# A hand-written schedule on one core: the planner's prices for VectorE and ScalarE, the hand-over between engines and the kernel product are changed

## The chip, the cores and the metric

The kernel runs on one core of a Trainium2 chip. The metric is the device time of one execution in microseconds (us), as the median of several. TensorE (PE) does the matrix products, VectorE (DVE) and ScalarE (ACT) work on what it leaves in PSUM, GpSimd (POOL) mostly starts DMAs and SyncE (SP) starts most of the others. Each engine executes its own instructions in the order in which they were written down, and waits on semaphores for the others.

## The reference, cut to what matters

There are 32 graphs of 512 nodes with 256 features. One layer is computed: a normalisation, then three things that feed a recurrent (GRU) cell, and the sum with the input.

```python
h = jnp.maximum(_layernorm(x, axis=-1), 0.0)
# convolution branch: 1 tap, then 17 taps along the nodes
c = jax.nn.relu(_bn(_conv1d(hc, conv1_w, 0), ...))
x_conv = jax.nn.relu(_bn(_conv1d(c, conv2_w, 8), ...) + hc)
# message branch
s = h @ w_se.T + b_se
A = jnp.exp(-dist(s, s)) * adj
x_nmp = jnp.einsum('bnm,bmd->bnd', A, jax.nn.relu(h @ w_msg.T + b_msg))
# gates
gi = concat([x_conv, x_nmp]) @ w_ih.T + b_ih
gh = h @ w_hh.T + b_hh
r, z = sigmoid(gi_r + gh_r), sigmoid(gi_z + gh_z)
out = x + (1 - z) * tanh(gi_n + r * gh_n) + z * h
```

All numbers are float32, and every matrix product is done in float32.

## The kernel before

**The work.** Five kinds of work share the engines. *Begins* normalise a graph and turn it so that features lie on partitions (`hT`), and store that in DRAM (`hd`). *Rows* load `hd` again into `hT`, do the one-tap convolution (`conv1`, PE into a bank `ps_g`, then ACT into `h`). *Conv* is the 17-tap convolution by a fast scheme: 7 groups of columns with 25 products each, 175 in all. DVE makes the operands `x` and `xd`, PE multiplies into the two banks `ps_c`, ACT copies them to `n` and `z`, DVE sums these into `y`, ACT writes `part` and a DMA stores it. *Graphs* make the messages, the matrix `A` and their product (`messages`, `factors`, `kernel_exp`, `masked`, `gather`). *Gates* do the GRU cell in banks `ps_acc`, most of it by Strassen's scheme.

**The order.** It is not left to a scheduler of the framework (`manual_schedule`). Each kind of work is a Python generator that issues a few instructions and then yields the time at which it can go on, or a condition. A planner at the end of the kernel keeps a clock `now`, which is PE's time: `matmul` adds `max(0.223, 0.005 + columns / 600)` us to it and `turn` adds 0.11. Of the generators that can go on, the planner picks the one whose stream is furthest behind, lets it issue, and calls `fill()`, which gives DVE and ACT background work as long as `dve.free < now + 1.5`. Where no generator can go on, `now` is moved by 0.25, and nothing is issued for it except, in the first stage, a transposition by the identity (`keep_warm`, line 147).

So no figure of the planner is a time on the chip. Figures decide only the order of instructions on the engines, and through it who waits.

**The figures.** `Engine` (lines 116 to 130) holds for DVE and ACT the time `free` at which the engine will be through with what it was given. An instruction moves it on:

```python
size = max(elements(t) for t in tiles if hasattr(t, "shape"))
self.free = max(self.free, now) + self.fixed + self.each * size
```

A generator that needs the result usually yields `act.free + LAG` or `dve.free + LAG`. Two places matter for what follows. After the first half of a product, `ps_c` is copied to the other bank by ACT, and the product goes on at `act.free + LAG`. When a product is done, `both` has ACT copy the two banks out one after the other, and what comes next on these banks may go on at `bank_at`, which is set after the first of the two copies:

```python
for k, half in enumerate(ps):
    n = half.shape[-1]
    act.activation(dst[:, k * n : (k + 1) * n], half, AF.Copy)
    if k == 0:
        bank_at = act.free + LAG
```

`kernel_exp` (line 966 and on) does four small matmuls at the same time, in four parts of the array (line 983); in the later stage its first bank is `pair[1]`, the second of the two banks. After them it moves `now` by a constant, and ACT takes the exponential of the four banks.

`load_row` (line 212) loads a graph's `hT` from DRAM; the rows yield until `now + 8.0`. DMA figures of this kind are constants and not touched by the change.

Of the kernel before, what the change touches and what calls it, by code (L numbers as in the profile page):

```python
# [50 lines left out]
def kernel(  # L51
# [31 lines left out]
    nc = tc.nc  # L83
# [22 lines left out]


    now = 5.0
    LAG = 0.6

    def elements(t):
        n = 1
        for k in t.shape[1:]:
            n *= k
        return n

    class Engine:
# [6 lines left out]
        def __getattr__(self, name):  # L124
            def issue(*tiles, **more):
                size = max(elements(t) for t in tiles if hasattr(t, "shape"))
                self.free = max(self.free, now) + self.fixed + self.each * size
                getattr(self.engine, name)(*tiles, **more)  # L128

            return issue  # L130

    dve, act = Engine(nc.vector, 0.12, 0.00108), Engine(nc.scalar, 0.16, 0.0009)

    def matmul(ps, lhsT, rhs, **more):
        nonlocal now
# [17 lines left out]
    def bank():  # L153
        return gps.tile([P, N], F32, name="ps_g")
# [4 lines left out]
    def later(t, f):  # L159
        LATER.append((t, f))  # L160
        LATER.sort(key=lambda e: e[0])
# [74 lines left out]
    def residual(b):  # L236
# [6 lines left out]
        def relu():  # L243
            act.activation(XC[b], XC[b], AF.Relu)
            RES[b] = act.free + LAG

# [104 lines left out]
    def norm(b):  # L351
# [14 lines left out]
        for c0 in range(0, NT, step):  # L366
# [5 lines left out]
            for c in range(c0, c0 + step):  # L372
# [4 lines left out]
                if c % 2:  # L377
                    yield act.free + LAG

# [156 lines left out]
    def weights_first():  # L536
# [10 lines left out]
        for j1 in ORDER:  # L547
# [12 lines left out]
            for j2 in ORDER:  # L560
# [13 lines left out]
                WS.append(w)  # L574
                W_AT.append(act.free + LAG)
                yield 0.0
# [24 lines left out]
    def third_weight(m):  # L601
# [5 lines left out]
        later(dve.free + 0.4, lambda: nc.gpsimd.dma_start(WD[m % 25][:, 2], w[2]))  # L607
        W_AT[m] = dve.free + LAG

# [11 lines left out]
    def summed(g):  # L621
# [23 lines left out]
        def both(dst, ps):  # L645
# [4 lines left out]
            else:  # L650
# [5 lines that stand above are left out]
            sums_at = act.free + LAG  # L656

# [314 lines left out]
    def kernel_exp(at):  # L972

        nonlocal now, bank_at, exp_waits
        exp_waits = False
        if not wide:
            extra = acc.tile([P, N], F32, name="ps_acc")
        else:
            extra = pair[1]
        pss = [extra, bank(), bank(), bank()]  # L980
        for c in range(NT):
            k = slice(32 * c, 32 * c + 5)
            nc.tensor.matmul(  # L983
                pss[c], gr.left[k, :], gr.right[k, :], start=True, stop=True,
                tile_position=(32 * c, 0),
            )
        now += 1.15
        for c in range(NT):
            act.activation(at[:, c, :], pss[c], AF.Exp)

# [95 lines left out]
    def graph(b):  # L1086
# [21 lines left out]
        if in_product:  # L1108
            exp_waits = True
            yield lambda: not in_product  # L1110
            yield bank_at
        kernel_exp(at)
        yield act.free + 0.3
        for n in range(NT):
# [593 lines left out]
```

## Time and profile before

The time is 2064.82 us, the median of 3 runs (2063.84 to 2067.84). The profiled execution took 2067.35 us, with a span of 2065.6 us from its first to its last instruction, so 1.75 us lie around the span; it is 2.5 us above the median.

| engine | busy us | share of the span | instructions |
|---|---|---|---|
| PE | 2012.4 | 97% | 9199 |
| DVE | 1416.3 | 69% | 2626 |
| ACT | 888.4 | 43% | 1805 |
| POOL | 451.1 | 22% | 578 |

| group of instructions | count | busy us |
|---|---|---|
| PE `ps_acc<-xnb,wih` | 772 | 364.4 |
| PE `ps_c<-xd,w` | 2304 | 291.8 |
| PE `ps_c<-x,w` | 2032 | 267.4 |
| PE `ps_g<-at,msg` | 512 | 227.1 |
| ACT `ps_c<-ps_c`, all widths | 144 | 56.1 |

How to read it: a float32 matmul stands in the records as two, so the program's 4796 matmuls and transpositions would be 9592 records, of which 9199 were kept. The mean granted clock of PE was 0.989 of full speed. The name to the left of `<-` is the tile that is written, those to the right are read. An instruction's recorded duration overlaps the next one on the same engine, so its spacing is shorter than its duration.

### The profile page before, as it was taken

How to read it: one execution, taken by the hardware profiler on the slowest of the kernel's cores; microseconds unless marked ns; L12 is line 12 of the kernel's file. 1: busy time of each engine (PE TensorE's matmuls, PEld its weight loads, DVE VectorE, ACT ScalarE, POOL GpSimd, SP SyncE). 2: the span in 40 equal slices, each digit the busy share in tenths (PEclk: the TensorE clock that was granted, in tenths of full speed). 3: DMA queues.
4: the chain of work that ended last, by engine and by line, in shares of the span. 5: the costliest groups of instructions: out<-in, count | busy, mean ns of one | idle time of the engine just before them, and what ended most of it. 6: DMA issues, size and time to landing. Idle time of an engine off the chain costs nothing. (4 is left out here: it accounts for less than half of the span.)

```text
span 2065.6 us, 27386 instructions
## 1 busy us (share of the span) xinstructions
PE 2012.4 (97%) x9199; PEld 1360.9 (66%) x9199; DVE 1416.3 (69%) x2626; ACT 888.4 (43%) x1805; POOL 451.1 (22%) x578
## 2 busy tenths in 40 slices
PE   8999889999999999999999999999999999999998
PEld 4878556676676766677577676667775677664444
DVE  6789378885878848687587775677875777752223
ACT  6554454335543445433454334554334633334221
POOL 2101022321212213122141221231221311114222
PEclk9999999999999999999999999999999999999999
DMA  7455668898979869778789788797886776756554
GB/s 286 150 174 184 225 209 196 192 226 226 223 197 203 190 192 205 201 182 212 183 193 223 172 204 206 164 197 204 207 204 175 189 158 159 173 118 143 63 92 36
DMA packets 581227, 378.70 MB, mean 183 GB/s; under 512 B 457648, under 2 KB 475344, under 8 KB 579952
## 3 DMA queue, kind: packets, MB, share of 16 engines
q1 hardware_dynamic: 419616, 279.02, 49.1%
q0 software_dynamic: 153184, 84.70, 23.9%
q10 hardware_dynamic: 8288, 13.24, 1.7%
q8 instruction: 73, 1.20, 0.2%
q14 instruction: 66, 0.54, 0.1%
HBM read 278.81 MB, written 114.56 MB: 190 GB/s over the span
## 5 line engine op out<-in xcount | busy, mean ns | idle before, releaser
L1218 POOL DMA_DIRECT2D out_dram<-o_sb x252 | 275.9, 1718 | 659.1 <-DVE o_sb L128 628.9
L137 PE MATMUL ps_acc<-xnb,wih 128*128 128x512 f32 (+1 forms) x772 | 364.4, 593 | 0.7 <-DVE ps_acc L128 0.7
L137 PEld LDWEIGHTS ps_c<-xd,w 128*128 128x128 f32 x2304 | 288.6, 191 | 55.0 <-issue 38.9
L137 PEld LDWEIGHTS ps_c<-x,w 128*128 128x128 f32 x2032 | 258.4, 193 | 72.3 <-issue 49.2
L137 PE MATMUL ps_c<-xd,w 128*128 128x135 f32 (+1 forms) x2304 | 291.8, 280 | 7.0 <-ACT ps_c L128 7.0
L137 PE MATMUL ps_c<-x,w 128*128 128x135 f32 (+2 forms) x2032 | 267.4, 281 | 11.4 <-ACT n L128 5.0
L137 PE MATMUL ps_acc<-hTb,whh 128*128 128x512 f32 (+2 forms) x580 | 239.5, 523 | 0.4 <-ACT r L128 0.4
L137 PE MATMUL ps_acc<-xconv,wih 128*128 128x512 f32 (+1 forms) x580 | 238.9, 519 | 0.3 <-DVE ps_acc L128 0.3
L137 PE MATMUL ps_g<-at,msg 128*128 128x512 f32 x512 | 227.1, 593 | 0.8 <-DVE at L128 0.8
L137 PEld LDWEIGHTS ps_acc<-xnb,wih 128*128 128x128 f32 x772 | 142.6, 191 | 115.6 <-issue 108.7
L137 PEld LDWEIGHTS ps_g<-at,msg 128*128 128x128 f32 x512 | 95.4, 190 | 106.4 <-issue 101.1
L137 PEld LDWEIGHTS ps_acc<-xconv,wih 128*128 128x128 f32 x580 | 107.6, 190 | 74.9 <-issue 67.5
L137 PEld LDWEIGHTS ps_acc<-hTb,whh 128*128 128x128 f32 x580 | 104.8, 191 | 78.6 <-issue 71.2
L128 DVE TENSOR_TENSOR msg<-ps_g,bmsg 128x256 f32<-128x256 f32 x128 | 53.7, 420 | 143.5 <-PE ps_g L137 143.1
L128 DVE SCALAR_TENSOR_TENSOR x<-x,x 128x544 f32<-128x544 f32 (+5 forms) x161 | 137.5, 854 | 2.9
L128 DVE TENSOR_TENSOR o_sb<-hTb,r 128x512 f32<-128x512 f32 x63 | 43.3, 687 | 124.1 <-ACT r L128 123.5
L128 ACT ACTIVATE ps_c<-ps_c 128x270 f32<-128x270 f32 (+1 forms) x144 | 56.1, 389 | 167.8 <-PE ps_c L137 167.8
L128 DVE TENSOR_TENSOR x<-x 128x272 f32<-128x272 f32 (+5 forms) x280 | 127.4, 497 | 0.2
L137 PE MATMUL ps_g<-hT,w 128*128 128x512 f32 (+8 forms) x296 | 122.1, 560 | 3.7 <-DMA hT<-hd 2.5
L137 PE MATMUL ps_g<-wmsg,hTg 128*128 128x259 f32 x496 | 123.5, 382 | 0.7 <-DVE aug L128 0.7
L128 ACT ACTIVATE h<-ps_g,bn_shift,bn_scale 128x252 f32<-128x252 f32 (+8 forms) x212 | 86.5, 485 | 73.2 <-PE ps_g L137 73.2
L128 DVE TENSOR_TENSOR xd<-x 128x544 f32<-128x544 f32 (+1 forms) x144 | 102.5, 716 | 14.0 <-PE ps_c L137 13.7
(149 smaller groups left out, 2927.5 us busy)
## 6 DMA issues: line engine op xcount, KB each, us to landing
w<-wd SPq DMA_DIRECT2D x414, 256.0 KB, 3.4
m_sb<-in_adj_dram SPq DMA_DIRECT2D x384, 64.0 KB, 3.8
hT<-hd SPq DMA_DIRECT2D x33, 512.0 KB, 4.4
hd<-hT POOLq DMA_DIRECT2D x32, 512.0 KB, 5.5
hTb<-hd SPq DMA_DIRECT2D x32, 512.0 KB, 4.6
xnb<-nd SPq DMA_DIRECT2D x64, 256.0 KB, 3.0
out_dram<-o_sb POOLq DMA_DIRECT2D x252, 64.0 KB, 4.9
hTg<-hd SPq DMA_DIRECT2D x31, 512.0 KB, 4.3
```

The costliest lines, as they stand in the source:

```text
L128: getattr(self.engine, name)(*tiles, **more)
L137: nc.tensor.matmul(ps, lhsT, rhs, **more)
L1218: nc.gpsimd.dma_start(dst, src, accum_op=ALU.add)
```

## The change

The figures by which the planner counts are replaced. `LAG`, the time from the end of an instruction on DVE or ACT to the moment at which another engine may count on its result, goes from 0.6 to 0.2 us. DVE's fixed part and its part per element go from 0.12 and 0.00108 to 0.066 and 0.00106, ACT's from 0.16 and 0.0009 to 0.05 and 0.00087; and each bias or scale that is given as a tile adds 0.1. After the four matmuls of `kernel_exp` the clock moves on by 1.5 in place of 1.15. No instruction is changed; their order is.

```diff
     now = 5.0
-    LAG = 0.6
+    LAG = 0.2
...
             def issue(*tiles, **more):
                 size = max(elements(t) for t in tiles if hasattr(t, "shape"))
-                self.free = max(self.free, now) + self.fixed + self.each * size
+                given = sum(hasattr(more.get(k), "shape") for k in ("bias", "scale"))
+                self.free = max(self.free, now) + self.fixed + self.each * size + 0.1 * given
                 getattr(self.engine, name)(*tiles, **more)
...
-    dve, act = Engine(nc.vector, 0.12, 0.00108), Engine(nc.scalar, 0.16, 0.0009)
+    dve, act = Engine(nc.vector, 0.066, 0.00106), Engine(nc.scalar, 0.05, 0.00087)
...
                 tile_position=(32 * c, 0),
             )
-        now += 1.15
+        now += 1.5
         for c in range(NT):
             act.activation(at[:, c, :], pss[c], AF.Exp)
```

## The prediction

> **What bounds the kernel now.** I read the page first: busy times, then the waits of PE, then the clock window by window, and last the rows around single waits.
>
> The page gives PE 97% of the span.
>
> ```profile
> span 2065.6 us, 27386 instructions
> PE 2012.4 (97%) x9199; PEld 1360.9 (66%) x9199; DVE 1416.3 (69%) x2626; ACT 888.4 (43%) x1805; POOL 451.1 (22%) x578
> ```
>
> PE is the bound, and the change takes no matmul away except 11 of the `keep_warm` transpositions (4796 to 4785 on PE; 11 x 0.11 = 1.2 us, issued only where PE has nothing else, so nothing). All that can move is where PE waits. PE's busy time by stretches (0 to 300, 300 to 1850, the rest) leaves 27.7, 19.0 and 6.9 us:
>
> ```profile
> 0.00:300.00 300.00, 272.31 (x1525) 201.64 (x1526) 216.18 (x476) 157.98 (x341) 40.11 (x80) 0.95 0.60 206
> 300.00:1850.00 1550.00, 1530.98 (x7177) 1065.47 (x7176) 1135.58 (x2064) 675.21 (x1393) 348.07 (x435) 0.99 0.81 193
> 1850.00:2066.00 216.00, 209.11 (x500) 93.83 (x498) 64.51 (x88) 55.19 (x73) 62.90 (x63) 1.00 0.52 82
> ```
>
> So the first 300 us lose most, the last 200 us nothing before the closing chain. Who is waited for after 300 us (total, times, longest):
>
> ```profile
> PE ps_c L983 <- ACT z L128: 6.7, 3, 4.0
> PE ps_c L137 <- ACT ps_c L128: 4.1, 4, 3.1
> PE ps_g L137 <- DMA hT<-hd: 2.5, 2, 1.2
> ```
>
> The kernel product waiting for the copy `z`, the second half of a product waiting for its copy, and the reload of `hT`. A long wait costs more than itself, as these stretches show (third number: PE busy; the number after POOL's: granted clock):
>
> ```profile
> 565.90:569.30 3.40, 1.20 (x8) 1.00 (x8) 3.30 (x6) 2.75 (x6) 0.90 (x2) 0.99 0.92 235
> 569.30:576.10 6.80, 4.64 (x18) 4.47 (x19) 6.70 (x12) 2.32 (x3) 5.58 (x8) 0.50 1.25 273
> 838.90:842.30 3.40, 0.00 (x0) 0.00 (x0) 3.37 (x3) 3.37 (x5) 3.40 (x4) 1.00 0.85 40
> 842.30:849.20 6.90, 6.83 (x18) 4.05 (x19) 4.41 (x8) 3.88 (x9) 0.25 (x1) 0.51 0.54 49
> ```
>
> After 3.4 us in which PE worked 1.20 or 0.00 us, the clock is 0.5 for 6.8 us: 3.4 us lost on top.
>
> **The change part by part.** *The prices themselves.* DVE instructions of 512 columns start 0.61 to 0.73 us apart in the trace (1006.05, 1006.77, 1007.50, 1008.11 us) and ACT's exponentials 0.49 apart. The old prices said 0.67 and 0.62, the new ones say 0.61 and 0.50. So the new durations are closer to the chip. They remove no work; what they and the smaller `LAG` do is to let PE come back sooner to a result, with less other PE work in between. How much lies in between I counted in the order of the built instructions, before and after, with a 512-column matmul at its spacing of 0.86 us (two records of 0.43).
>
> *First term: nine kernel products that come too early.* In the changed order, 9 kernel products stand one matmul (0.86 us) after the transpositions of their right factor while ACT has still to do `right` and then both copies of a finished product; before, such products had two matmuls (1.72 us) or more. The reason is that `bank_at` is set after the first copy and the kernel product needs the second bank. The old 0.6 covered the second copy, the new 0.2 doesn't. The rows of such a wait:
>
> ```profile
> 784.34 0.68 ACT L128 ACTIVATE z<-ps_c 128x270 f32<-128x270 f32 x2 [2.46 <-DVE y L128]
> 785.08 0.69 PE L983 MATMUL ps_c<-right,left 5*128 5x512 f32 x1 [2.23 <-ACT z L128]
> ```
>
> From the first copy's start to PE's start are 0.74 us. Before that come 0.20 from PE's end to ACT's start and 0.49 for `right` (836.68 to 837.17): 1.43 us, against 0.86 of cover. 9 x 0.57 = **+5.1 us** (2.5 to 6).
>
> *Second term: reloads of `hT`.* A row's `hT` is read from DRAM where the graph's `hd` has just been written. The rows yield for 8.0 us, and the chain is longer (start, length):
>
> ```profile
> 1349.21 4.73 DMA hd<-hT
> ...
> 1353.96 3.56 DMA hT<-hd
> ```
>
> This one made PE wait 1.22 us, another 1.23. In the order before, two reloads plainly have less PE work between the last work ahead of `hd` and the first `conv1` matmul than the chain takes; in the changed order it is seven, because rows come sooner behind the transposition that makes `hT`. 5 x 1.22 = **+6.1 us** (0, if the writes land a little faster or POOL is free; 15, if POOL's adds to `out`, 4.4 us for four, stand ahead of `hd` each time).
>
> *Third term: the copy inside a product.* Here the order changes most: of 144 such copies, 8 had one matmul of cover and 74 had two; now 86 have one and 22 have two. The need, from rows:
>
> ```profile
> 1778.87 1.08 PE L137 MATMUL ps_c<-x,w 128*128 128x135 f32 x8
> ...
> 1780.05 0.38 ACT L128 ACTIVATE ps_c<-ps_c 128x270 f32<-128x270 f32 x1 [0.26 <-PE ps_c L137]
> ...
> 1780.48 0.73 PE L137 MATMUL ps_c<-xd,w 128*128 128x135 f32 x4 [0.53 <-ACT ps_c L128]
> ```
>
> The half product takes 8 x 0.115 = 0.92 us and ends at 1779.79; PE goes on 0.69 us later. One matmul covers that with 0.17 to spare, so as such the edit costs nothing. The cover that hides it is that ACT has nothing else in hand; ACT's copies `n` and `z` wait for DVE 40.7 us in all by their groups (19.0, 11.2, 7.0 and 3.5), 2% of the span, and a hand-over that hits such a wait now lacks one matmul of cover, up to 0.86 us: 86 x 2% x 0.6 = **+1 us** (0 to 9).
>
> *Fourth term: long waits after 300 us.* The order there is another, so those before go: 1.74 and 3.07 us (565 to 571), 2.23 (783), 4.01 (838), 11.1 in all, and two stretches at half clock, 6.8: -17.9 us. Others come. The worst, a third of the way into the second group of columns: DVE's transposition of the next `hT` waits for the last `conv1` matmul that reads the buffer, and behind it on DVE are queued `xd`, a `y` sum, the second transposition and the third weight `w`, for which PE waits: 0.63 + 0.64 + 1.76 + 0.63 + 0.60, with 0.3 for the two hand-overs 4.6 us, under 0.87 us of messages, so 3.7. Just before, a pair of `conv1` matmuls waits 1.2 for its bank, and that much idle time together costs the half clock, 3.4: 8.3. Three more places, where PE waits behind ACT's `part` or DVE's queue, lack 1.8, 1.75 and 2.5 us: 6.1. -17.9 + 8.3 + 6.1 = **-3.5 us** (-14 if the new ones prove covered; +8 if each new one brings the half clock).
>
> The rule of the Trainium skill in "TensorE: Matmul & The Clock Gate", section "Why this matters for your kernels", allows idle gaps of up to some 3 us and counts a full idle window for the fall to half clock. The stretch at 565.90, with 1.20 us of work, fell too. By that rule only the worst of the new waits could fall and the fourth term would keep its lower half; by the row, several can.
>
> *Fifth term: the first 300 us.* Gone: four waits from 255 to 278 us (2.08, 0.74, 2.00, 2.87) and the one at 208 (2.49), with half clock after two of them, 6.8: -17.0. New: hand-overs that lack 2.0 to 2.6 us at five places, 11.6, and one half clock, 3.4. **-2 us** (-9 to +6).
>
> *`now += 1.5`.* Four such matmuls take PE 1.07 us in the rows (785.08 to 786.15), so the planner's clock now runs ahead by 0.43 for each of the 32 graphs, and ACT and DVE are given that much more work than they have time for. Their slack of 31% and 57% takes it up; it is in the terms above where it matters.
>
> Sum: 5.1 + 6.1 + 1 - 3.5 - 2 = +6.7 us. The profiled execution, 2067.35, would become 2074.0; it lies 2.5 above the median, so the median of 2064.8 becomes 2071.5.
>
> **The rivals.** *It is faster* (0.27). Accurate prices might place work so that the long waits go and do not come back. The mechanism is the clock: four stretches at half clock (208, 255, 565, 838) cost 13.6 us, and a schedule whose waits stay under about 2 us in any 3.4 pays none. With the reloads covered (second term 0) and the worst new wait alone left, the sum is 5.1 + 1 - 17.9 + 8.3 - 5 = -8.5: 2056. It decides if `hd` lands in 4.0 us rather than 4.73, and no two new waits fall together. For it: waits of 4 us and more vanish from the order. Against: by the same count over the order, places where PE comes sooner than the chain before it allows rise from 33 to 51.
>
> *No change that can be told* (0.26). The terms have both signs and 3 us less in the second and third bring the sum to within 4 us: 2061 to 2069.
>
> *The change doesn't do what it says* (part of the slower side, 0.13). The figures are then too short, not traced: for the copy in a product the planner now counts 0.29 + 0.20 = 0.49 us where the rows show 0.69. If the 86 short covers are hit more often than 2%, say one in five by 0.5 us, that is 9 us in place of 1, and 2080.
>
> **How the numbers follow.** Slower, by the sum above or by more, has 0.47, no change 0.26, faster 0.27; under 0.2%, 4.1 us, a measurement of this kernel can't tell a change from none. The time is that of the sum, 2071.5. The range takes the bounds of the terms as independent: downwards 2.6, 6, 1, 10.5 and 7, together 14.3; upwards 1, 9, 8, 11.5 and 8, together 18.6. It is drawn in a little at the top, where only the rival of short figures reaches: 2057 to 2085. The slower case alone would be 2069 to 2086.
>
> **What would show it.** Right: PE's waits for `z` and `n` at line 983 rise from 3 to about 10, most of them near 0.6 us; the waits on the DMA `hT<-hd` rise from 2 to between 4 and 7; the copy `ps_c` is rarely waited for in spite of its short cover; a wait of 3 us or more and a half clock stand near 450 us. Wrong: line 983 not among PE's waits, or the clock at full speed all through after 300 us with a PE idle time there below 15 us, which would make it the faster rival; or dozens of small waits on `ps_c`, which would make it the rival of short figures.

## The result, and the profile after

The changed kernel takes 2090.01 us (median of 5 runs, 2086.88 to 2091.11), the kernel before beside it 2067.33 us (2063.84 to 2073.49): a ratio of 1.0107, with a 95% interval of 1.0086 to 1.0127. It is slower, by 22.7 us and not by the forecast 6.7, and 5 us above the range.

The profiled execution took 2090.64 us. Page, busy times:

```profile
span 2088.9 us, 27331 instructions
PE 2022.3 (97%) x9188; PEld 1356.1 (65%) x9188; DVE 1417.3 (68%) x2626; ACT 888.3 (43%) x1797; POOL 448.8 (21%) x578
```

The work of DVE and ACT is what it was; no engine has become a new bound. (The diff adds a line ahead of all these places: L137 is now L138, L128 is L129, L983 is L984.) The windows, PE's busy time first:

```profile
0.00:300.00 300.00, 276.55 (x1529) 200.87 (x1530) 218.53 (x463) 158.53 (x340) 40.12 (x81) 0.96 0.61 205
300.00:1850.00 1550.00, 1513.42 (x7073) 1048.18 (x7072) 1125.47 (x2053) 667.60 (x1369) 342.41 (x433) 0.99 0.81 191
1850.00:2089.00 239.00, 232.39 (x588) 107.00 (x586) 73.31 (x111) 62.16 (x88) 66.25 (x68) 1.00 0.53 86
```

In the first 300 us PE does 4.2 us more than before; in the next 1550 us it does 17.6 less, and a closing stretch 23 us longer is what that costs. So the loss lies after 300 us. There PE is idle for 36.6 us instead of 18.9, and half clock costs 13.7 us instead of 8.5 (each stretch of 3.4 us by the part of the clock that was not granted). PE's waits after 300 us, total, times and longest:

```profile
PE ps_acc L138 <- ACT r L129: 5.9, 4, 5.3
PE ps_g L138 <- DMA hT<-hd: 5.6, 3, 3.2
PE ps_acc L138 <- DVE ps_acc L129: 4.7, 6, 1.7
PE ps_c L138 <- ACT z L129: 4.5, 1, 4.5
PE ps_c L984 <- ACT z L129: 3.3, 8, 0.5
PE ps_c L138 <- ACT ps_c L129: 3.1, 4, 1.5
PE ps_c L984 <- ACT n L129: 2.1, 3, 1.5
```

The kernel product (L984) waits 11 times for 5.4 us, mostly 0.40 each: a small share. The two longest waits, 5.3 and 4.5 us, are for ACT. What held ACT up is in the timeline around the longer one (start, duration, in brackets the idle time before it and who ended it):

```profile
1350.51 4.47 POOL L1219 DMA_DIRECT2D out_dram<-o_sb  x4
...
1352.12 1.34 ACT L129 ACTIVATE part<-y,bn_shift,bn_scale 128x522 f32<-128x522 f32 x1
...
1353.25 2.90 POOL L746 DMA_DIRECT2D cd<-part  x2
...
1360.89 1.00 ACT L129 ACTIVATE part<-y,bn_shift,bn_scale 128x360 f32<-128x360 f32 x1 [6.16 <-DMA cd<-part]
...
1362.91 0.69 ACT L129 ACTIVATE r<-ps_acc,vec 128x512 f32<-128x512 f32 x1
...
1363.65 2.93 PE L138 MATMUL ps_acc<-hTb,whh 128*128 128x512 f32 x3 [5.27 <-ACT r L129]
```

`part` has two buffers. ACT was through with the older one at 1349.67 (start 1348.33, 1.34 us). POOL issues its store only at 1353.25, after four adds to `out` have been started, and it lands at 1360.87, 11.2 us after ACT was through with the buffer. The next `part` waits 6.2 us for that buffer, and `r`, the gate for which PE waits, comes after it on ACT. The planner counts 5.0 us for that store (`PARTS.append(act.free + 5.0)`). At 575.08 it is the same with `z`: `part` waits 5.62 us, then come 4.47 us of `y`, then `z`. ACT's waits for this store, before and after, from the two lists of waits:

```profile
ACT part L128 <- DMA cd<-part: 12.7, 16, 3.0
```

```profile
ACT part L129 <- DMA cd<-part: 29.8, 13, 6.2
```

### The profile page after: what moved, and what is told of

Same layout as the page of the kernel before. It is cut to its first block, busy times and chain, and to the rows that moved or that the text cites. A ratio compares the mean times of both kernels' runs of the same rounds, so it can differ in the third digit from the quotient of the medians.

```text
span 2088.9 us, 27331 instructions
## 1 busy us (share of the span) xinstructions
PE 2022.3 (97%) x9188; PEld 1356.1 (65%) x9188; DVE 1417.3 (68%) x2626; ACT 888.3 (43%) x1797; POOL 448.8 (21%) x578
## 4 chain that ended last, share of the span: by engine, by line
PE 44%; DVE 2%; DMA 2%; issue 1%; POOL 1%; ACT 1%; SPq 0%; DVEq 0%; POOLq 0%; ACTq 0%
PE ps_acc L138 26%; PE ps_c L138 9%; PE ps_g L138 8%; DMA hd<-hT 1%; PE ps_c L984 1%; POOL out_dram L1219 0%; DMA xconv<-cd 0%; DMA hT<-hd 0%; DMA cd<-part 0%; DVE o_sb L129 0%; DVE z L129 0%; POOL cd L746 0%; DVE y L129 0%; PE ps_g L143 0%; DVE st L129 0%
## 5 line engine op out<-in xcount | busy, mean ns | idle before, releaser
L138 PE MATMUL ps_acc<-xnb,wih 128*128 128x512 f32 (+1 forms) x772 | 366.0, 592 | 0.3 <-DVE ps_acc L129 0.2
L138 PEld LDWEIGHTS ps_c<-xd,w 128*128 128x128 f32 x2304 | 285.0, 190 | 54.4 <-ACT ps_c L129 34.0
L138 PEld LDWEIGHTS ps_c<-x,w 128*128 128x128 f32 x2032 | 258.9, 193 | 71.6 <-issue 42.3
L138 PE MATMUL ps_c<-xd,w 128*128 128x135 f32 (+1 forms) x2304 | 291.0, 279 | 3.3 <-ACT ps_c L129 3.1
L138 PE MATMUL ps_c<-x,w 128*128 128x135 f32 (+2 forms) x2032 | 268.5, 281 | 11.0 <-ACT z L129 5.5
L138 PE MATMUL ps_acc<-hTb,whh 128*128 128x512 f32 (+2 forms) x580 | 242.4, 525 | 5.9 <-ACT r L129 5.9
L138 PE MATMUL ps_acc<-xconv,wih 128*128 128x512 f32 (+1 forms) x580 | 240.3, 520 | 1.8 <-DVE ps_acc L129 1.8
L138 PE MATMUL ps_g<-at,msg 128*128 128x512 f32 x512 | 234.2, 607 | 7.3 <-DVE at L129 7.3
L138 PEld LDWEIGHTS ps_acc<-xnb,wih 128*128 128x128 f32 x772 | 140.7, 190 | 109.0 <-issue 101.6
L138 PEld LDWEIGHTS ps_g<-at,msg 128*128 128x128 f32 x512 | 97.8, 195 | 121.2 <-issue 107.7
L138 PEld LDWEIGHTS ps_acc<-hTb,whh 128*128 128x128 f32 x580 | 104.6, 191 | 82.0 <-issue 69.7
L138 PEld LDWEIGHTS ps_acc<-xconv,wih 128*128 128x128 f32 x580 | 106.5, 190 | 75.6 <-issue 66.0
L129 DVE TENSOR_TENSOR msg<-ps_g,bmsg 128x256 f32<-128x256 f32 x128 | 53.8, 421 | 147.3 <-PE ps_g L138 146.9
L129 DVE SCALAR_TENSOR_TENSOR x<-x,x 128x544 f32<-128x544 f32 (+5 forms) x161 | 137.8, 856 | 3.3
L138 PE MATMUL ps_g<-hT,w 128*128 128x512 f32 (+8 forms) x296 | 127.6, 578 | 12.2 <-DMA hT<-hd 9.0
L129 ACT ACTIVATE ps_c<-ps_c 128x270 f32<-128x270 f32 (+1 forms) x144 | 56.0, 389 | 172.6 <-PE ps_c L138 172.6
L138 PE MATMUL ps_g<-wmsg,hTg 128*128 128x259 f32 x496 | 125.8, 384 | 1.7 <-ACT h L129 1.1
L129 DVE TENSOR_TENSOR x<-x 128x272 f32<-128x272 f32 (+5 forms) x280 | 126.9, 499 | 0.2
L129 DVE TENSOR_TENSOR o_sb<-hTb,r 128x512 f32<-128x512 f32 x63 | 43.2, 686 | 113.2 <-ACT r L129 113.2
L129 ACT ACTIVATE h<-ps_g,bn_shift,bn_scale 128x252 f32<-128x252 f32 (+8 forms) x212 | 86.8, 484 | 71.6 <-PE ps_g L138 71.5
L138 PEld LDWEIGHTS ps_g<-wmsg,hTg 128*128 128x128 f32 x496 | 92.3, 191 | 33.3 <-issue 20.3
```

What stands on the lines that cost most here:

```text
L138: nc.tensor.matmul(ps, lhsT, rhs, **more)
```

## The experiments

**Theory and rivals.** The theory formed after the result: it is `LAG`. The old 0.6 us was not only the time from engine to engine; it was also cover for three waits that the planner does not describe: the second copy of `both` ahead of a kernel product (`bank_at` is set after the first), the `part` store behind POOL's adds, and the reload of `hT`, whose write and read take longer than the counted 8.0 us. Rival one: the new durations, or the 1.5 us after `kernel_exp`, cost the time. Rival two: any other order is worse than the old one, which was a lucky draw, and no figure matters by itself.

In the tables, "idle" is PE's idle time after 300 us (in brackets the waits of over 1.4 us), "half clock" what the clock took there, and "`part`" ACT's waits for its store, all from the profile, all in us. Ratios are to the kernel before.

| run | us | ratio (95%) | idle | half clock | `part` |
|---|---|---|---|---|---|
| before | 2067.33 | 1 | 18.9 (11.0) | 8.5 | 12.7 |
| after | 2090.01 | 1.0107 (1.0086 to 1.0127) | 36.6 (21.7) | 13.7 | 29.8 |
| lag06 | 2079.35 | 1.0059 (1.0041 to 1.0076) | 32.9 (22.1) | 11.9 | 24.7 |
| lagonly | 2094.67 | 1.0128 (1.0100 to 1.0155) | 39.2 (29.3) | 18.8 | 18.4 |
| exp115 | 2090.37 | 1.0126 (1.0092 to 1.0160) | 33.9 (23.7) | 13.7 | 13.4 |

### Which figure costs the time

*lag06*: the changed kernel with the old `LAG`, so the new durations and the 1.5 alone.

```diff
-    LAG = 0.2
+    LAG = 0.6
```

> The changed kernel with LAG back at 0.6 us; the new prices and the 1.5 after the kernel product stay. Theory of thin cover (the short hand-over takes the PE work away from between a result and its use): the 23 us come back but for what 1.5 and the prices cost, 2065 to 2072 us, and the eleven waits of 0.4 us at the kernel product are gone. Theory of undescribed waits (ACT's part behind its store, hT behind its write, which no figure covers): little comes back, 2080 to 2090, since prices and not LAG put the part earlier. Theory of a lucky order before (any other figures give a worse order): anything from 2065 to 2095, without relation to the edit.

*lagonly*: the kernel before with the new `LAG` alone.

```diff
-    LAG = 0.6
+    LAG = 0.2
```

> The kernel before with LAG 0.2 us alone; prices and 1.15 as before. Theory of thin cover: most of the loss is here, 2080 to 2092 us, softened a little since the old prices are some 10% too long on DVE and hold PE back by themselves. If the prices carry the loss: 2065 to 2072. Lucky order: no relation, 2065 to 2095.

*exp115*: the changed kernel with the old step after `kernel_exp`.

```diff
-        now += 1.5
+        now += 1.15
```

> The changed kernel with 1.15 in place of 1.5 after the kernel product. The rows show 1.07 us, so the planner's clock runs ahead less. If the constant matters, ACT and DVE are less behind and the time falls by 5 us or more, to below 2085; if it does not, 2086 to 2094. Lucky order: anything within 15 us of 2090, up as well as down.

`lagonly` loses all of it and more, 1.28%; giving the old `LAG` back (`lag06`) brings half of the loss back and no more. Neither time is in the range that the theory of thin cover gave it: 2094.67 lies above 2080 to 2092, and 2079.35 above 2065 to 2072. The middle window of `lagonly` shows where its loss is:

```profile
300.00:1850.00 1550.00, 1511.41 (x7044) 1050.49 (x7043) 1125.75 (x2053) 665.21 (x1372) 342.23 (x431) 0.99 0.81 191
```

PE does 19.6 us less there than before (1530.98), as in the changed kernel. Its waits for `hT` are not more than before (1.6 us against 2.5), so its loss is not one of waits for the reloads. `exp115` changes nothing in the time, though it changes the waits much: the kernel product's waits go from 5.4 to 20.3 us and those for `part` from 29.8 to 13.4. Taking the 1.5 back brings nothing back. The 12 us of `lag06` were left open here: a price of the new durations, or of this one order.

### Describing the three waits

*guards*: the changed kernel, with all three waits given to the planner: the kernel product yields until after the second copy (`sums_at`), the store counts 9.0 us, the reload 11.0.

```diff
-            HR_AT[b] = now + 8.0
+            HR_AT[b] = now + 11.0
...
-        PARTS.append(act.free + 5.0)
+        PARTS.append(act.free + 9.0)
...
-            yield bank_at
+            yield sums_at
         kernel_exp(at)
```

> The changed kernel with three waits described that its figures leave out: the kernel product may go on only after the second copy (sums_at in place of bank_at in graph), a part buffer counts as free 9 us after the evacuation in place of 5, and a reload of hT is due 11 us after its issue in place of 8. Theory of undescribed waits: the 11 waits at the kernel product (5.4 us idle), most of ACT's 29.8 us on the stores of part and PE's 9.0 us on hT go, with half of the half clock: 2065 to 2073 us. Theory of thin cover at large: only those places get better, 2075 to 2085. Lucky order: 2070 to 2095 with new waits at other places.

*g_parts*, *g_reload* and *g_kernel*: the changed kernel with one of these three edits each (the 9.0, the 11.0, and `sums_at`).

> The changed kernel with one of the three waits described: a part buffer counts as free 9 us after the evacuation, not 5. In the changed kernel ACT stood 29.8 us behind stores of part, and PE's two longest waits (4.5 and 5.3 us) with two stretches of half clock and smaller ones came from that. Theory of undescribed waits: ACT's wait on these stores falls below 5 us, PE's waits of 4.5 and 5.3 us go, 2073 to 2080 us. Theory that any change of the order draws a new lot (lucky order before): the stores' wait may go, but the time stays within 2080 to 2098 with other waits.

> The changed kernel with a reload of hT due 11 us after its issue, not 8. Theory of undescribed waits: PE's 9.0 us on hT go below 2, with one stretch of half clock, 2079 to 2084 us. New lot: 2070 to 2098, whatever becomes of the waits on hT.

> The changed kernel with the kernel product held until the second copy too. Theory of undescribed waits: the 11 waits of about 0.4 us at that line (5.4 us) go, 2083 to 2087 us. New lot: 2070 to 2098; the 11 waits go all the same, but other waits decide the time.

*b_guards*: the kernel before with all three.

> The kernel before (LAG 0.6, old prices, 1.15) with all three waits described. Its ACT stood 12.8 us behind the stores of part and its PE 2.5 us on hT, so there is less to win than in the changed kernel. Theory of undescribed waits: 2060 to 2067 us. New lot: 2065 to 2095, as with any other order.

| run | us | ratio (95%) | idle | half clock | `part` |
|---|---|---|---|---|---|
| guards | 2066.29 | 0.9992 (0.9980 to 1.0004) | 29.8 (14.5) | 10.2 | 0.8 |
| g_parts | 2082.01 | 1.0079 (1.0057 to 1.0100) | 31.8 (17.3) | 11.9 | 1.7 |
| g_reload | 2075.89 | 1.0037 (1.0021 to 1.0054) | 33.3 (17.4) | 11.9 | 29.9 |
| g_kernel | 2068.03 | 1.0002 (0.9991 to 1.0014) | 25.3 (12.9) | 5.1 | 28.5 |
| b_guards | 2070.36 | 1.0007 (0.9997 to 1.0017) | 21.0 (11.6) | 10.2 | 1.3 |

With all three edits, the new figures cost nothing any more: 2066.3 against 2090.0. ACT no longer waits for its store, and PE does 7 us more in the middle window than in the changed kernel:

```profile
ACT part L129 <- DMA cd<-part: 0.8, 2, 0.4
```

```profile
300.00:1850.00 1550.00, 1520.14 (x7125) 1053.63 (x7124) 1132.34 (x2053) 671.90 (x1377) 341.25 (x430) 0.99 0.81 192
```

PE's waits for `hT` fall from 9.0 to 0.9 us. Those of the kernel product for its bank `ps_c`, though, do not fall: 6 of them for 6.6 us, one of 4.2, against 11 for 5.4. The same edits do nothing at the old figures (`b_guards`, though its `part` waits too fall from 12.7 to 1.3), so they are worth something only beside the new ones. That speaks for the theory, although it had expected 2060 to 2067 there. More speaks against reading it too neatly. All three single edits miss the range that the theory gave them. They bring 8, 14 and 22 us, 44 in all, where together they bring 24. `g_kernel` alone brings 22 though it can take away only the 5.4 us of waits at L984 and their share of the clock (5 of them for 2.0 us are left); its waits for `part` stay at 28.5 and those for `hT` at 8.4. (`g_reload` does to the reloads what it says: 3 waits for 2.5 us are left.) Each edit also draws a new order, and that is worth some us by itself. How many was measured next.

### The figure, or one order

A figure was moved by little: enough for another order, too little for another meaning. `b_lag058` and `b_lag062` are the kernel before, `a_lag018` and `a_lag022` the changed one, `p_lag058` and `p_lag08` the changed one with larger values.

```diff
-    LAG = 0.6
+    LAG = 0.58      # b_lag058; 0.62 in b_lag062
...
-    LAG = 0.2
+    LAG = 0.18      # a_lag018; 0.22, 0.58 and 0.8 in the others
```

> The kernel before with LAG 0.58 in place of 0.6 us, an edit that describes the chip neither better nor worse, but reorders PE from its first stage on. Theory of systematic figures (what the prices and LAG say decides): within 5 us of before, 2063 to 2073. Theory of a lucky order before (each order is a new lot, and the kernel before is one of the better ones): 2070 to 2090, as lag06 with 2079.

> The kernel before with LAG 0.62. Systematic figures: 2063 to 2073. Lucky order: 2070 to 2090, and not the same as with 0.58.

> The changed kernel with LAG 0.18 in place of 0.2 us. Systematic figures: within 5 us of 2090. New lot: 2066 to 2095, away from 2090 by more than 5 us as likely as not, since the one-word edit at the kernel product gave 2068.

> The changed kernel with LAG 0.22. Systematic figures: within 5 us of 2090. New lot: 2066 to 2095, and not the same as with 0.18. If both of these lie near 2090 and both of before's neighbours near 2067, the lot is refuted.

> New prices and 1.5 with LAG 0.58, neighbour of the run with 0.6 (2079). If the new prices lose by themselves (they take the ten per cent away by which DVE was counted too slow): 2074 to 2084, like that run. If that run was an unlucky neighbour and LAG is all: 2065 to 2073.

> New prices and 1.5 with LAG 0.8. Theory of thin cover, with the sum of price and LAG as what counts: 0.2 more for each hand-over gives back what the shorter prices took (0.06 on DVE, 0.11 on ACT), so 2063 to 2072. If the prices lose in another way (DVE's and ACT's queues filled too full, which LAG can't mend): 2074 to 2085.

| run | us | ratio (95%) | idle | half clock | `part` |
|---|---|---|---|---|---|
| b_lag058 | 2070.24 | 1.0006 (0.9993 to 1.0018) | 17.8 (11.8) | 10.2 | 26.1 |
| b_lag062 | 2070.71 | 1.0006 (0.9995 to 1.0018) | 21.1 (12.4) | 10.2 | 19.1 |
| a_lag018 | 2085.27 | 1.0079 (1.0060 to 1.0098) | 34.9 (21.8) | 17.1 | 36.3 |
| a_lag022 | 2097.62 | 1.0135 (1.0118 to 1.0151) | 37.2 (22.5) | 17.1 | 16.5 |
| p_lag058 | 2066.88 | 0.9989 (0.9980 to 0.9998) | 22.6 (9.7) | 8.5 | 14.8 |
| p_lag08 | 2068.90 | 1.0001 (0.9988 to 1.0013) | 25.7 (14.8) | 11.9 | 29.4 |

Two of the middle windows side by side, `b_lag058` first, then `a_lag022`:

```profile
300.00:1850.00 1550.00, 1532.19 (x7182) 1066.09 (x7181) 1136.94 (x2066) 675.26 (x1397) 349.31 (x436) 0.99 0.81 193
```

```profile
300.00:1850.00 1550.00, 1512.71 (x7068) 1047.27 (x7068) 1127.08 (x2056) 664.07 (x1368) 343.43 (x431) 0.99 0.80 191
```

The kernel before was no lucky draw: its neighbours are within 0.1% of it. Around 0.2 all three orders lose, by 0.8 to 1.35%, and `lagonly` and `exp115` with them, so the loss belongs to the figure; its size, between 2085 and 2098 us, is a draw. And with the new durations a `LAG` of 0.58 or 0.8 loses nothing, so the 12 us of `lag06` were that one order's, not the durations'. Rival one falls; of rival two there remains the scatter.

What the larger `LAG` covers is less clear than the theory has it. ACT's waits for the store of `part` do not go with the time: `b_lag058` and `p_lag08` have 26.1 and 29.4 us of them and lose nothing, `a_lag022` has 16.5 and is the slowest of all. The longest wait of the changed kernel, for `r` behind `part`, stands in `p_lag058` too, and longer than there:

```profile
PE ps_acc L138 <- ACT r L129: 6.1, 1, 6.1
ACT part L129 <- DMA cd<-part: 14.8, 11, 7.0
```

So a `LAG` of 0.58 did not cover this wait, and a kernel that has it can still be as fast as the one before.

### The described waits at other values

*gk_018* and *gk_022* are `g_kernel` at 0.18 and 0.22, *gd_022* and *gd_04* are `guards` at 0.22 and 0.4.

```diff
-            yield bank_at
+            yield sums_at
...
-    LAG = 0.2
+    LAG = 0.18      # gk_018; 0.22 in gk_022; with the 9.0 and 11.0 too, 0.22 in gd_022 and 0.4 in gd_04
```

> The kernel product held until the second copy, with LAG 0.18. If the hold itself wins the 22 us that it won with 0.2, since PE then has other work where the kernel product stood: 2063 to 2075, against 2085 without it. If 2068 was one order out of a wide scatter, and the hold wins only its 5 us: 2078 to 2092.

> The same with LAG 0.22, where the time without the hold was 2098. The hold itself: 2068 to 2080. One order out of a scatter: 2085 to 2100.

> All three waits described, LAG 0.22, where none described gave 2098 and the held kernel product alone 2090. If the waits that the figures leave out are what a short hand-over uncovers: 2064 to 2074, as with LAG 0.2 (2066). If 2066 was a good draw: 2078 to 2095.

> All three waits described, new prices, LAG 0.4, between the two figures. With cover for what is still left out and accurate prices this should be no worse than before and may beat both kernels: 2058 to 2067. If it scatters as the orders near 0.2 do: 2068 to 2085.

| run | us | ratio (95%) | idle | half clock | `part` |
|---|---|---|---|---|---|
| gk_018 | 2069.62 | 1.0005 (0.9993 to 1.0016) | 26.0 (15.2) | 8.5 | 24.8 |
| gk_022 | 2090.17 | 1.0103 (1.0082 to 1.0125) | 32.6 (16.8) | 8.5 | 17.5 |
| gd_022 | 2067.64 | 0.9994 (0.9985 to 1.0004) | 21.0 (8.4) | 1.7 | none |
| gd_04 | 2049.88 | 0.9914 (0.9893 to 0.9935) | 13.7 (2.0) | 1.7 | 0.5 |

The second copy alone is not the cause: its edit brings 22 us at 0.2, 16 at 0.18 and 7 at 0.22, and at 0.22 the kernel still loses 1%. All three together bring the time back at 0.2 and at 0.22, by 24 and 30 us. That is the evidence for the three edits as a set. How much of it is each one's own stays open, and so does whether it is the described waits at all: the same extra time at places where no wait was found was not tried, and it might have served as cover just as well.

With the three described and a `LAG` between the old and the new, `gd_04` beats both kernels, by 0.86%. Its page, its middle window, PE's waits after 300 us, and ACT's wait for the store:

```profile
span 2045.2 us, 27388 instructions
PE 2001.7 (98%) x9188; PEld 1351.3 (66%) x9188; DVE 1419.1 (69%) x2626; ACT 888.6 (43%) x1801; POOL 449.6 (22%) x578
```

```profile
300.00:1850.00 1550.00, 1536.30 (x7205) 1063.70 (x7202) 1147.49 (x2072) 680.89 (x1394) 351.78 (x443) 1.00 0.82 194
```

```profile
PE ps_acc L138 <- ACT ps_acc L129: 4.7, 5, 2.0
PE ps_c L138 <- ACT n L129: 3.5, 4, 1.3
PE ps_c L138 <- ACT ps_c L129: 1.5, 3, 0.5
```

```profile
ACT part L129 <- DMA cd<-part: 0.5, 1, 0.5
```

No wait for `hT` or `part` is left among the long ones, only one of 2.0 us is over 1.4, and the granted clock of the window is 1.00. No neighbour of `gd_04` was run, so how much of its gain is this one order's is open.

## Why the prediction was wrong

The direction and three of the terms stood. The step that failed is the fourth term; that the miss of the whole is about as large as its miss is luck, since two further errors cancel.

- **First term, kernel products (+5.1): right in sum.** 11 waits at line 984, 5.4 us, mostly 0.40 each and one of 1.5, where nine at 0.57 were forecast.
- **Second term, `hT` (+6.1): right in sum.** The whole run has 5 waits for 9.0 us, before it had 2 for 2.5: +6.5. They are fewer and longer than forecast, up to 3.2 us.
- **Third term, the copy inside a product (+1): right.** 4 waits in both, 3.1 us against 4.1. `gd_04` shows it best: by the order of its instructions 78 of its copies have one matmul of cover, and after 300 us all its waits for these copies come to 1.5 us. The rival of short figures named this place for its 9 us; its direction was right and its place wrong.
- **Fifth term, the first 300 us (-2): right in direction, too small.** Idle time goes from 27.7 to 23.4 us, although the reloads, which the second term counts, take 3.4 more of it than before; and half clock costs 1.8 us less. Without the reloads that is -9.5, just outside the term's own -9 to +6.
- **Fourth term, long waits after 300 us (-3.5): this step failed.** Without the kernel product and the reloads, PE's waits for ACT and DVE there went from 9.4 to 25.4 us, +16.0, and half clock added 5.2. The waits at line 983 that the term took away count 7.0. So the third and fourth terms together measure +14.2 where they were forecast at -2.5. That is 16.7 too little, and the miss of the whole is 16.0 (22.7 against 6.7). The two agree only because 7.5 us that the fifth term had too high stand against 6.5 us that no term has: of the 23.3 us by which the profiled spans differ, 6.5 are in PE's busy records beyond the half clock. With their share of it, `ps_g<-at,msg` takes 7.1 us more than before and `ps_g<-hT,w` 5.5; the cause is open.

What the runs showed in the fourth term's place: its worst new wait, near 450 us, was there with its half clock, but as three gaps of 1.06, 1.07 and 1.28 us, 3.4 of idle time and not 4.9. The large new waits were two others, 4.48 and 5.27 us, for ACT, whose `part` had itself waited 5.6 and 6.2 us for a store behind POOL's other DMAs. With the half clock after them, 1.7 and 3.4 us, the two come to 14.9 us. The term's three further places, 1.8, 1.75 and 2.5 us, "behind ACT's `part` or DVE's queue", name no DMA for which `part` would wait; the record does not say where they were, so whether these two waits are among them is open. The second term weighed POOL's adds in front of `hd`, and the fourth did not weigh the same adds in front of `cd<-part`. Nearly all that was to show the prediction right was there, about ten waits at the kernel product, the reloads, few waits for the copy and a half clock near 450 us; but none of these signs looked at waits behind `part`.

The range is a miss of its own. The bounds as added up reach 2071.5 + 18.6 = 2090.1, which still holds the 2090.0; it was drawn in to 2085 in the belief that only the rival of short figures reaches higher. And the faster rival's condition, that waits under about 2 us in any 3.4 cost no half clock, does not hold in the kernel before: its clock fell at 1576 us though PE's records fill 3.37 of the 3.40 us ahead (last section).

That the closer prices did not help is no contradiction: with a `LAG` of 0.58 or 0.8 they lose nothing. It is `LAG` that had two jobs, the hand-over and a cover for what the planner leaves out, and only the hand-over was traced. That it has the second job follows from the orders near 0.2: all five lose as they stand, and neither of the two with the three edits does. Which waits it covers is not shown.

## What to carry to other kernels

A slack constant in a planner can cover waits that the planner does not describe; before it is cut to the traced hand-over, list those waits (a second instruction on the same bank, a buffer whose store stands behind another engine's queue, a write and a read through DRAM) and give each its own time. When an order is rewritten by a figure, run the figure's neighbours before an experiment is believed: here 0.02 us of `LAG` moved the time by as much as 22 us (`g_kernel` to `gk_022`), by 12 at the old `LAG` with the new durations (`p_lag058` to `lag06`), and by less than 4 around the kernel before. And a forecast of new waits made from an order bounds only the waits that it finds, each without the DMA behind it unless that is counted too, so its upper end needs room for the others.

## What was not expected of the hardware

How PE's idle time leads to half clock is not settled by its length. Windows of the changed kernel (third number PE's busy time, the one after POOL's the granted clock):

```profile
451.40:454.80 3.40, 1.44 (x9) 0.95 (x7) 0.86 (x2) 1.83 (x6) 0.00 (x0) 1.00 0.68 266
455.30:455.80 0.50, 0.50 (x2) 0.41 (x2) 0.50 (x1) 0.00 (x0) 0.00 (x0) 0.50 0.00 0
```

```profile
692.30:695.70 3.40, 0.24 (x1) 0.00 (x0) 1.85 (x3) 1.39 (x5) 0.00 (x0) 1.00 0.90 242
696.70:698.70 2.00, 2.00 (x6) 0.95 (x5) 0.00 (x0) 0.94 (x3) 0.00 (x0) 1.00 1.08 208
```

At 455 the clock fell after 3.4 us in which PE had worked 1.44 us; at 692 it did not fall after 3.4 us with 0.24. The Trainium skill, in "TensorE: Matmul & The Clock Gate", section "Why this matters for your kernels", allows idle gaps of up to some 3 us. The second pair, with a gap of 3.2 us, about fits that; the first does not, as gaps of 1.06 and 1.07 us with work between them were enough. The kernel before has a fall behind a stretch that PE's records fill almost wholly:

```profile
1572.80:1576.20 3.40, 3.37 (x11) 1.02 (x10) 0.00 (x0) 3.40 (x10) 0.73 (x1) 1.00 0.44 154
1576.20:1579.60 3.40, 3.40 (x10) 2.24 (x10) 0.00 (x0) 0.82 (x2) 0.00 (x0) 0.50 0.27 69
```

Nearly all of PE's work in the first of these two rows is one graph's kernel product, whose operands fill 5 partitions in place of 128. In the changed kernel the fall at 1561 comes behind a kernel product too, with PE busy for 3.14 of 3.40 us. Whether such a product counts as work for the clock, and what decides in the other cases, was not tried. For a forecast it means that two waits of about 1 us close together can cost as much on top as one of 4 us, and that the idle time alone does not foretell the half clock.
